# A graph network stack on one core: the ranking stage's lists carry two f32 values per node in place of five bf16 values

## The chip, the cores and the metric

The kernel runs on one core of a Trainium2 chip, as one launch. The metric is the device time of that core in microseconds (us), read as the median of several executions. The core has five engines with instruction streams of their own: TensorE (PE, matmuls; its weight loads are shown apart as PEld), VectorE (DVE), ScalarE (ACT), GpSimd (POOL) and SyncE (SP, which here issues transfers). Each works through its own stream in order and waits on semaphores of the others.

## The reference

Four graph layers with residuals over 2708 nodes with 128 features. Only the second layer matters here:

```python
h = jnp.maximum(_layernorm(x, axis=-1), 0.0)
x = x + _L1_gnn_ref(h, adj, L1_gnn_W, L1_gnn_a)

def _L1_gnn_ref(X, A, W, a):
    XW = jnp.matmul(X, W)
    f = W.shape[1]
    s_col = jnp.matmul(XW, a[0, :f])
    s_row = jnp.matmul(XW, a[0, f:])
    Z1 = jax.nn.leaky_relu(s_row[:, None] + s_col[None, :], negative_slope=0.01)
    den = jnp.exp(Z1)
    num = jnp.matmul(A, den)
    att = jnp.where(num != 0, den / jnp.where(num != 0, num, 1.0), 0.0)
    H = jnp.matmul(A, jnp.matmul(att, XW))
    return H
```

`num` is a product of two 2708 x 2708 matrices, but `den` depends on a pair of nodes only through the sum of two numbers, and the leaky ReLU has one kink. So for a column the rows fall into two groups, those whose `s_row` is above minus `s_col` and those below. If the rows are sorted by `s_row`, `num` follows from running sums over the sorted rows.

## The kernel before

The 2708 nodes are T = 22 tiles of P = 128 (the last has 20). The kernel runs layer 0, then the **ranking stage** of layer 1, then the **knots stage** (running sums over sorted rows of the adjacency, written to a table in DRAM), then a stage that gathers pairs of table rows and forms the attention, then layers 2 and 3. Almost every instruction around the change goes through `pe`, `dve` or `act` (line 86), wrappers that keep an engine's instructions in the order of the text; in the profile they all carry line L84, so groups are told apart by their tiles. The order of the ranking stage is thus written out by hand, in the loop at lines 1527 to 1572.

**The ranking stage.** `row_all` holds all nodes' row terms along the free axis, `r_nat` the same numbers by tile and partition. For tile `t`:

- `mask(t)` (DVE, line 1344) writes a bf16 mask of the nodes behind this one whose term is not larger. `masks` live in `flags`, a pool of three buffers, so `mask(t)` waits until `counts(t-3)` and `summed(t-3)` have read theirs.
- `counts(t)` (PE, line 1379) adds the mask's columns into the PSUM tiles `cnt`, 512 columns a bank, with bf16 matmuls of 32 columns of ones.
- `summed(t)` (ACT, line 1372) adds the mask along its row into `later`, writing a copy that nobody reads into `seen`; three tiles (2, 19, 20) do it on DVE inside `mask`.
- Every four tiles `count_row(b)` (ACT) copies a finished bank's row out of PSUM, `count_turn(b)` (PE) turns it into a column by four transposes, and `ranked(b)` (DVE) forms the rank of each node of the group, after the column is there.
- `listed(t0, t1)` (DVE, line 1454) turns ranks into a tile number and a place in that tile and writes, per node, a one-hot row over tiles (`in_tile`, 22 wide), a one-hot row over places (`in_place`, 131 wide) and the first multiplied by the node's values `vals` (`in_tile_v`). They are held in `in_spare` for tiles 0 to 15 (eight at a time) and in the buffer `lists` for tiles 16 to 21.
- `joined(t0, t1)` (PE, line 1482) multiplies, for each tile, the one-hot places (as weights) with `in_tile_v`, and adds into the PSUM tile `sp`: this scatters each node's values to its rank. It does so in two matmuls a tile: one whose weights are the last three columns of `in_place` (`DUP`; they carry knots to the next tile's start) and one whose weights are the first 128.
- `totals(n)` (PE, line 1251) takes the next `n` row tiles of the adjacency and adds their weighted rows, as f32 matmuls with 32 weight columns, eight a tile. This is a separate sum over all rows that needs no ranking; its tiles are spread over the loop by the table `TOTALS`, and the last one is done after `weights(0)` (line 1663).

A value is an f32 number, so before the change it is carried as bf16 pieces: the node number as partition and tile (`vals` 0 and 1), and the row term `r_n` as three bf16 terms whose sum is the number (`vals` 2 to 4, made on POOL by `split_terms`, line 1518). `sp` has `LIST = 5 * T = 110` columns and starts from `empty`, constants for the places that no node fills.

**Behind the loop** (lines 1564 to 1572): `listed(12, 16)`, `ranked(4)`, `listed(16, 20)`, `count_row(5)`, `count_turn(5)`, `ranked(5)`, `listed(20, T)`, `joined(12, T)`. Then DVE puts the pieces together into `src_u` (which row of the adjacency comes at which place) and `rs` (its row term), and POOL's queue gathers the adjacency's rows in sorted order: `fetch(t)` (line 1604), an indirect transfer of 1354 KB a tile into `mov`. POOL computes nothing of weight here; its queue holds these gathers in order. `rs` goes through three exponentials on ACT into the weights `wt` of the knots stage.

**The knots stage** (line 1755) multiplies each gathered tile with `wt`, copies the result to SBUF and writes it to `table`; SP issues those writes, and `fetch(t + 3)` the gather of a later tile.

Of the kernel before, what the change touches and what calls it, by code (L numbers as in the profile page):

```python
# [17 lines left out]
P = 128  # L18
# [6 lines left out]
def kernel(  # L25
# [18 lines left out]
    nc = tc.nc  # L44
    N, D = x.shape
    assert D == P
    T = -(-N // P)
# [25 lines left out]
    def pin(ins):  # L73

        return tc.keep_in_program_order(ins)
# [188 lines left out]
    nc.vector.memset(at_place[:, P + 2 :], float(PER))  # L264
    at_tile = consts.tile([P, T], F32, name="at_tile")
    nc.gpsimd.iota(at_tile, [[1, T]], base=0, channel_multiplier=0, allow_small_or_imprecise_dtypes=True)
    own_id = consts.tile([P, T], F32, name="own_id")
    nc.gpsimd.iota(own_id, [[0, T]], base=0, channel_multiplier=1, allow_small_or_imprecise_dtypes=True)
    vals = consts.tile([P, 5, T], BF16, name="vals")
    nc.vector.tensor_copy(vals[:, 0, :], own_id)  # L270
    nc.vector.tensor_copy(vals[:, 1, :], at_tile)
    empty = consts.tile([P, 5, T], BF16, name="empty")
    nc.vector.memset(empty, 0.0)
    for v, first, fill in ((1, 3, float(P // 2)), (2, 2, -1e5)):
        nc.gpsimd.affine_select(
            out=empty[:, v, :], in_=empty[:, v, :], pattern=[[0, T]],
            compare_op=ALU.is_ge, fill=fill, base=-first, channel_multiplier=1,
        )
        nc.gpsimd.affine_select(
            out=empty[:, v, :], in_=empty[:, v, :], pattern=[[-PER, T]],  # L280
            compare_op=ALU.is_ge, fill=fill, base=N + 2, channel_multiplier=-1,
        )
    nc.vector.scalar_tensor_tensor(
        empty[:, 2, 0:1], ident[:, 2:3], 88.0, empty[:, 2, 0:1], op0=ALU.mult, op1=ALU.add
    )
    source = consts.tile([P, 2], F32, name="source")
    nc.vector.tensor_scalar(
# [355 lines left out]
    for c in range(len(COLS) - 2):  # L643
        t0, t1 = COLS[c]
# [331 lines left out]
    def vec(name, n=T, dt=F32):  # L976
        return keep.tile([P, n], dt, name=name)
# [215 lines left out]
    nc.gpsimd.memset(later[:, T - 1 :], 0.0)  # L1193
    nc.gpsimd.memset(rank[:, T - 1 :], 0.0)
    hi, rmax, part = vec("hi", 1), vec("rmax", 1), vec("part", 1)
    r_n, w_n = vec("r_n"), vec("w_n")
    sp = acc(4)
    LIST = 5 * T
    q0, e4, e5 = KBS[E3][0], range(*GROUPS[E4]), range(*GROUPS[E5])
    copy_h(E3 - 1, last_turn[0])  # L1200
    roots(E3)
# [70 lines left out]
    def front_total():  # L1272
# [5 lines left out]
    totals(1)  # L1278
    terms_turned(E3 - 1)
    pe.matmul(  # L1280
        sp[:, :LIST], ident_b, empty.rearrange("p v t -> p (v t)"), start=True, stop=False
    )
    rows_p = ps_s.tile([P, 512], F32, name="ps")
    turn_h(E3, rows_p)
# [49 lines left out]
    cnt = [ps_s.tile([P, 512], F32, name="ps") for _ in range(2)]  # L1334


    lists = lay.tile([P, 2 * N], BF16, name="lists", tag="H")
    seen = lists[:, :N]

    SUMMED_HERE = (2, T - 3, T - 2)  # L1340
    own_later = {t: vec(f"own_later{t}", 1) for t in SUMMED_HERE}
# [30 lines left out]
    def summed(t):  # L1372
        w, a = width(t), t * P
        if t not in SUMMED_HERE:
            act.activation(
                seen[:w, a:], masks[t][:w, a:], AF.Copy, accum_out=later[:w, t : t + 1]
            )
# [55 lines left out]
    def in_spare(first):  # L1433
        box(
            first,
            8,
            (
                spare.tile([P, 8, T], BF16, name="in_tile"),
                spare.tile([P, 8, P + 3], BF16, name="in_place"),
                spare.tile([P, 5, 8, T], BF16, name="in_tile_v"),  # L1440
            ),
        )

    def in_lists(first, n):
        o = N
        made = []
        for shape, size in (("(i t) -> i t", n * T), ("(i t) -> i t", n * (P + 3)), ("(v i t) -> v i t", 5 * n * T)):
            kw = dict(i=n) if shape[1] == "i" else dict(v=5, i=n)
            made.append(lists[:, o : o + size].rearrange("p " + shape.replace("-> ", "-> p "), **kw))
            o += size  # L1450
        assert o <= 2 * N
        box(first, n, made)

    def listed(t0, t1):

        n = t1 - t0
        (ta, pl, tv), i = boxes[t0]
        r_, a_, m_ = rank[:, t0:t1], tile_of[:, t0:t1], at_of[:, t0:t1]
        dve.tensor_scalar(a_, r_, -(PER + 1) / 2.0, 1.0 / PER, op0=ALU.add, op1=ALU.mult)
        dve.tensor_scalar(a_, a_, 1.5 * BIG, None, op0=ALU.add)  # L1460
        dve.tensor_scalar(a_, a_, -1.5 * BIG, None, op0=ALU.add)
        dve.scalar_tensor_tensor(m_, a_, -float(PER), r_, op0=ALU.mult, op1=ALU.add)
        dve.tensor_tensor(
            ta[:, i : i + n, :],
            at_tile[:, None, :].to_broadcast([P, n, T]),
            a_[:, :, None].to_broadcast([P, n, T]),
            ALU.is_equal,
        )
        dve.tensor_tensor(
            pl[:, i : i + n, :],  # L1470
            at_place[:, None, :].to_broadcast([P, n, P + 3]),
            m_[:, :, None].to_broadcast([P, n, P + 3]),
            ALU.is_equal,
        )
        dve.tensor_tensor(
            tv[:, :, i : i + n, :],
            ta[:, None, i : i + n, :].to_broadcast([P, 5, n, T]),
            vals[:, :, t0:t1, None].to_broadcast([P, 5, n, T]),
            ALU.mult,
        )  # L1480

    def joined(t0, t1):
        for t in range(t0, t1):
            (_, pl, tv), i = boxes.pop(t)
            w = width(t)
            pe.matmul(
                sp[:3, :LIST].rearrange("p (v t) -> p v t", t=T)[:, 2:, 1:],
                pl[:w, i, DUP],
                tv[:w, 2:, i, : T - 1],
                start=False,  # L1490
                stop=False,
            )
            pe.matmul(
                sp[:, :LIST], pl[:w, i, :P], tv[:w, :, i, :], start=False, stop=(t == T - 1)
            )
# [19 lines left out]
        act.activation(s_n, c_n, AF.Exp, scale=0.99)  # L1515
        act.activation(sig, hb, AF.Exp)

    def split_terms():
        parts_of_r = keep.tile([P, 2, T], F32, name="parts_of_r")
        pin(nc.gpsimd.tensor_copy(vals[:, 2, :], r_n))  # L1520
        pin(nc.gpsimd.tensor_tensor(parts_of_r[:, 0, :], r_n, vals[:, 2, :], ALU.subtract))
        pin(nc.gpsimd.tensor_copy(vals[:, 3, :], parts_of_r[:, 0, :]))
        pin(nc.gpsimd.tensor_tensor(parts_of_r[:, 1, :], parts_of_r[:, 0, :], vals[:, 3, :], ALU.subtract))
        pin(nc.gpsimd.tensor_copy(vals[:, 4, :], parts_of_r[:, 1, :]))

    TOTALS = {6: 2, 7: 2, 10: 2, **{t: 1 for t in (0, 1, 2, 3, 8, 9, 12, 13, 14, 16, 18)}}
    for t in range(T):
        mask(t)
        if t == 1:
            split_terms()  # L1530
        if t == 7:
            ranked(0)
        if t == 8:
            column_max()
        if t == 10:
            ranked(1)
            in_spare(0)
            listed(0, 8)
        if t == 11:
            node_terms()  # L1540
        if t == 14:
            ranked(2)
            in_spare(8)
            listed(8, 12)
        if t == 18:
            ranked(3)
        counts(t)
        if t in (7, 11, 15):
            count_row(t // 4)
        summed(t)  # L1550
        if t == 4:
            front_total()
        if t in (3, 19):
            count_row(t // 4)
        if t % 4 == 0 and t:
            count_turn(t // 4 - 1)
        if t == 11:
            joined(0, 8)
        if t == 15:
            joined(8, 12)  # L1560
        if t in (2, 3, 4, 5):
            column_terms(t)
        totals(TOTALS.get(t, 0))
# [3 lines left out]
    listed(16, 20)  # L1567
    count_row(5)
    count_turn(5)
    ranked(5)  # L1570
    listed(20, T)
    joined(12, T)
# [6 lines left out]
    def signs_of(t):  # L1579
# [10 lines left out]


    src_u, rs = vec("src_u", dt=U32), vec("rs")
    ids = vec("ids")
    dve.tensor_copy(ids, sp[:, :T])
    dve.scalar_tensor_tensor(
        src_u, sp[:, T : 2 * T], float(P), ids, op0=ALU.mult, op1=ALU.add
    )
    dve.tensor_copy(rs, sp[:, 4 * T : 5 * T])
    dve.tensor_tensor(rs, sp[:, 3 * T : 4 * T], rs, ALU.add)
    dve.tensor_tensor(rs, sp[:, 2 * T : 3 * T], rs, ALU.add)  # L1600

    moving = {}

# [32 lines left out]
    nc.vector.tensor_copy(wt[:, :, 0], pw)  # L1636
    nc.vector.tensor_copy(wt[:, :, 1], nw)

    below = spare.tile([P, 4, P], F32, name="below", tag="below")
    for g in range(4):  # L1640
        dve.tensor_copy(below[:, g, :], ident[:, 32 * g : 32 * g + 1].to_broadcast([P, P]))
    dve.memset(below[:, :, 0:1], 0.0)
# [390 lines left out]
```

## Time and profile before

| what | value |
|---|---|
| median of 3 runs | 1090.12 us (1088.93 to 1092.9) |
| the profiled execution: its own time | 1095.87 us |
| the profiled execution: span of its instructions | 1094.2 us |
| mean granted TensorE clock in it | 0.968 of full speed |
| PE busy over the span | 994.4 us (91%), 3561 instructions |
| DVE, ACT, POOL busy | 586.0, 402.8, 214.1 us |
| moved by DMA | 282.72 MB, 258 GB/s over the span |
| ranking loop to the first gather of the knots stage | about 416 us to 463.8 us of the span |

The profiled execution is a single one and is 5.75 us longer than the median of the three that were timed; differences of a microsecond are read inside it, not between it and the others. In the profile an f32 matmul appears as two MATMUL records (and two weight loads), a bf16 matmul and a transpose as one. A timeline row merges neighbouring instructions of one kind: start, length, engine, line, operation, the tiles written and read, shapes (weights' rows and columns, then partitions by moving columns), how many records, and in brackets how long the engine was idle before it and what ended that.

### The profile page before, as it was taken

To read this page: it belongs to the slowest core of one execution; us is meant where nothing else is said; L and a number is where in the kernel's file an instruction comes from. 1 tells how busy PE (TensorE), PEld (TensorE's weight loads), DVE (VectorE), ACT (ScalarE), POOL (GpSimd) and SP (SyncE) were. 2 spreads that over 40 slices of the span, in tenths; PEclk is the share of its full clock that TensorE was granted. 3 is DMA by queue.
4 is the path that set the end of the run, shared out by engine and by line. 5 is a ranking of instruction groups with operands and counts; after the bars stand their busy time and mean duration, and the time that the engine had idled before them with its cause. 6 is when DMAs were issued, how large, how long until landed. Compare 5 with 4: busy or idle time off the path is not lost.

```text
span 1094.2 us, 10202 instructions
## 1 busy us (share of the span) xinstructions
PE 994.4 (91%) x3561; PEld 486.0 (44%) x3561; DVE 586.0 (54%) x1208; ACT 402.8 (37%) x637; POOL 214.1 (20%) x242
## 2 busy tenths in 40 slices
PE   6999999999899999899798288778999999999998
PEld 5445444444344445554343133333444545554444
DVE  4365368999863276856475499989300311031003
ACT  5100045544300058579675377878100310021000
POOL 2000000000188741023232155551000000000000
PEclk9999999999999998999999669999999999999999
DMA  9987220004399439399999899998999167716801
GB/s 272 347 318 234 89 68 16 0 1 153 123 363 405 159 128 413 143 382 425 419 421 388 308 431 431 432 431 350 425 352 410 75 229 279 255 51 224 301 36 51
DMA packets 48083, 282.72 MB, mean 258 GB/s; under 512 B 6238, under 2 KB 17594, under 8 KB 28420
## 3 DMA queue, kind: packets, MB, share of 16 engines
q1 hardware_dynamic: 38191, 189.13, 45.9%
q0 software_dynamic: 9840, 92.94, 20.9%
q8 instruction: 28, 0.46, 0.2%
q14 instruction: 24, 0.20, 0.0%
HBM read 250.06 MB, written 33.00 MB: 259 GB/s over the span
## 4 chain that ended last, share of the span: by engine, by line
PE 64%; DMA 22%; DVE 8%; ACT 2%; issue 2%; POOL 1%; SPq 0%; DVEq 0%; POOLq 0%; ACTq 0%
PE acc L404 31%; PE acc L84 16%; DMA pair<-table,pair_u 11%; PE acc L806 10%; DMA mov<-in_adj_dram,src_u 6%; DMA chunk<-in_adj_dram 3%; DVE att L84 3%; PE ps L84 3%; PE ps L384 1%; DVE top_i L843 1%; DMA held<-in_adj_dram 1%; PE acc L814 1%; ACT sg L1582 1%; DVE mov L84 1%; DMA w<-in_L_gnn_W_dram 1%
## 5 line engine op out<-in xcount | busy, mean ns | idle before, releaser
L84 PE MATMUL acc<-att,xw 128*128 128x512 f32 (+3 forms) x264 | 111.6, 577 | 51.4 <-DVE att L84 51.4
L404 PE MATMUL acc<-chunk,h 128*128 128x512 f32 (+1 forms) x384 | 148.0, 542 | 0.0
L84 PE MATMUL acc<-mov,wt 128*128 128x512 f32 (+1 forms) x264 | 111.0, 568 | 18.1 <-DVE mov L84 16.1
L806 PE MATMUL acc<-zT 128*128 128x512 f32 (+2 forms) x264 | 112.3, 559 | 0.0
L404 PEld LDWEIGHTS acc<-chunk,h 128*128 128x128 f32 x384 | 68.8, 190 | 74.1 <-issue 74.1
L84 PEld LDWEIGHTS acc<-att,xw 128*128 128x128 f32 (+1 forms) x264 | 50.6, 199 | 112.4 <-issue 81.8
L947 POOL DMA_INDIRECT gath<-ydr,near_u x63 | 60.3, 957 | 154.4 <-DMA ydr<-y 140.6
L84 PEld LDWEIGHTS acc<-mov,wt 128*128 128x128 f32 x264 | 48.0, 194 | 80.5 <-DVE mov L84 39.8
L404 PE MATMUL acc<-chunk,y 128*128 128x512 f32 x204 | 80.0, 553 | 3.8 <-DMA chunk<-in_adj_dram 3.0
L821 ACT COPY strip<-acc 128x512 f32<-128x512 f32 (+1 forms) x132 | 60.4, 560 | 59.2 <-issue 35.8
L1805 POOL DMA_INDIRECT pair<-table,pair_u x22 | 66.6, 3026 | 75.7 <-DVE att L84 63.8
L84 DVE SCALAR_TENSOR_TENSOR att<-pair,kap 128x2708 f32<-128x2708 f32 (+3 forms) x28 | 67.7, 2433 | 23.1 <-DMA pair<-table,pair_u 23.1
L84 DVE COPY mov<-knots 2x512 f32<-2x512 f32 x126 | 47.6, 402 | 51.1 <-DMA mov<-in_adj_dram,src_u 25.8
L404 PE MATMUL acc<-chunk,attended 128*128 128x512 f32 x192 | 73.6, 543 | 0.4 <-DMA chunk<-in_adj_dram 0.4
L84 ACT ACTIVATE att<-att,sca 128x2708 f32<-128x2708 f32 (+3 forms) x28 | 57.8, 2065 | 37.6 <-DVE att L84 37.6
L823 DVE MAX8 top_v<-strip 128x8 f32<-128x2708 f32 (+1 forms) x22 | 64.7, 2966 | 7.3 <-ACT strip L821 7.3
L806 PEld LDWEIGHTS acc<-zT 128*128 128x128 f32 (+1 forms) x264 | 45.1, 185 | 51.3 <-issue 43.8
L84 DVE SCALAR_TENSOR_TENSOR att<-row_all,inv_s,att 128x2708 f32<-128x2708 f32 (+3 forms) x28 | 67.6, 2428 | 0.4 <-ACT att L84 0.4
L84 ACT ACTIVATE att<-att,hb 128x2708 f32<-128x2708 f32 (+3 forms) x28 | 57.9, 2068 | 0.9
L404 PEld LDWEIGHTS acc<-chunk,y 128*128 128x128 f32 x204 | 37.2, 193 | 45.8 <-issue 41.3
L1582 ACT ACTIVATE sg<-row_all,c_nat 128x2708 bf16<-128x2708 f32 (+1 forms) x22 | 56.4, 2564 | 0.1
L84 ACT COPY knots<-acc 128x512 f32<-128x512 f32 x66 | 37.3, 594 | 42.0 <-PE acc L84 40.8
(381 smaller groups left out, 1267.2 us busy)
## 6 DMA issues: line engine op xcount, KB each, us to landing
chunk<-in_adj_dram SPq DMA_DIRECT2D x75, 1354.0 KB
table<-knots SPq DMA_DIRECT2D x19, 1354.0 KB
res<-in_adj_dram SPq DMA_DIRECT2D x9, 1354.0 KB
held<-in_adj_dram SPq DMA_DIRECT2D x11, 512.0 KB
held<-in_adj_dram SPq DMA_DIRECT2D x16, 256.0 KB
upper<-in_adj_dram SPq DMA_DIRECT2D x4, 842.0 KB
held<-in_adj_dram SPq DMA_DIRECT2D x3, 1024.0 KB
chunkY<-in_adj_dram SPq DMA_DIRECT2D x2, 1354.0 KB
```

The source lines that it names most:

```text
L84: return lambda *a, **k: pin(getattr(self.engine, name)(*a, **k))
L384: mm = nc.tensor.matmul(p[: width(t), t - t0, :], srcT[:, cols(t)], w, start=True, stop=True)
L404: nc.tensor.matmul(out[b][:, :n], y[r, tile_at(i), :], chunk(i)[r, k0 : k0 + n], start=(i == 0), stop=(i == T - 2),)
L806: mm = nc.tensor.matmul(zz[b][:w, :n], zT[:, cols(t)], zT[:, k0 : k0 + n], start=True, stop=False)
L814: nc.tensor.matmul(zz[b][:w, :n], ones_b[g : g + 3, :w], sq_rows[g : g + 3, k0 : k0 + n], start=False, stop=True,)
L821: copied = nc.scalar.copy(s[:w, k0 : k0 + n], zz[b][:w, :n])
L823: nc.vector.max(top_v[:w, t, :], s[:w, :])
L843: pin(nc.vector.max_index(top_i[:w, t, :], top_v[:w, t, :], strips[t][:w, :]))
L947: nc.gpsimd.indirect_dma_start(out=g[: idx.shape[0], :], out_offset=None, in_=ydr[:, :], in_offset=bass.IndirectOffsetOnAxis(ap=idx, axis=0),)
L1582: nc.scalar.activation(sg[:w, :], row_all[:w, :], AF.Sign, bias=c_nat[:w, t : t + 1], accum_out=signs[:w, t : t + 1],)
L1805: nc.gpsimd.indirect_dma_start(out=r[:w].rearrange("p a n -> p (a n)"), out_offset=None, in_=table[:, :], in_offset=bass.IndirectOffsetOnA ...
```

## The change

- **Values.** `vals` becomes two f32 numbers per node: the node number `128 t + p`, made by one iota, and `r_n`, which is now written in place (`r_n = vals[:, 1, :]`). `split_terms` and the two copies and the iota that made the bf16 pieces are gone. `empty` and `LIST` shrink with it (2 x 22 = 44 columns of f32 in place of 110 of bf16).
- **Lists.** `in_tile`, `in_place` and `in_tile_v` are f32; `lists` keeps its bytes, its lower half now holds the f32 lists and its upper half `seen`. `in_place` and the later `below` share a buffer.
- **Matmuls.** `joined` and the matmul that starts `sp` are f32 matmuls: 44 and 21 moving columns in place of 110 and 63.
- **Behind it.** `src_u` is one DVE instruction on PSUM (it adds 0.25 before the conversion) in place of two, `rs` one copy in place of a copy and two additions.
- **Order.** `count_row(2)` and `count_row(3)` stand behind `summed(11)` and `summed(15)` in ACT's order, where they stood ahead; `count_row(1)` stays ahead. The totals tile that was taken at t = 18 is taken behind `count_turn(5)`, ahead of `ranked(5)`, `listed(20, T)` and `joined(12, T)` in the text. SP's order of transfers is the same.

```diff
-    vals = consts.tile([P, 5, T], BF16, name="vals")
-    nc.vector.tensor_copy(vals[:, 0, :], own_id)
-    nc.vector.tensor_copy(vals[:, 1, :], at_tile)
-    empty = consts.tile([P, 5, T], BF16, name="empty")
+    vals = consts.tile([P, 2, T], F32, name="vals")
+    nc.gpsimd.iota(vals[:, 0, :], [[P, T]], base=0, channel_multiplier=1, allow_small_or_imprecise_dtypes=True)
+    empty = consts.tile([P, 2, T], F32, name="empty")
...
-    r_n, w_n = vec("r_n"), vec("w_n")
+    r_n, w_n = vals[:, 1, :], vec("w_n")
     sp = acc(4)
-    LIST = 5 * T
+    LIST = 2 * T
...
-        sp[:, :LIST], ident_b, empty.rearrange("p v t -> p (v t)"), start=True, stop=False
+        sp[:, :LIST], ident, empty.rearrange("p v t -> p (v t)"), start=True, stop=False
...
-    lists = lay.tile([P, 2 * N], BF16, name="lists", tag="H")
-    seen = lists[:, :N]
+    lists = lay.tile([P, N], F32, name="lists", tag="H")
+    seen = lists[:, N // 2 :].bitcast(BF16)
+    wide = lists[:, : N // 2]
...
-                spare.tile([P, 8, T], BF16, name="in_tile"),
-                spare.tile([P, 8, P + 3], BF16, name="in_place"),
-                spare.tile([P, 5, 8, T], BF16, name="in_tile_v"),
+                spare.tile([P, 8, T], F32, name="in_tile"),
+                spare.tile([P, 8, P + 3], F32, name="in_place", tag="in_place"),
+                spare.tile([P, 2, 8, T], F32, name="in_tile_v"),
...
-            ta[:, None, i : i + n, :].to_broadcast([P, 5, n, T]),
-            vals[:, :, t0:t1, None].to_broadcast([P, 5, n, T]),
+            ta[:, None, i : i + n, :].to_broadcast([P, 2, n, T]),
+            vals[:, :, t0:t1, None].to_broadcast([P, 2, n, T]),
...
-                sp[:3, :LIST].rearrange("p (v t) -> p v t", t=T)[:, 2:, 1:],
+                sp[:3, T + 1 : LIST],
                 pl[:w, i, DUP],
-                tv[:w, 2:, i, : T - 1],
+                tv[:w, 1, i, : T - 1],
...
-    TOTALS = {6: 2, 7: 2, 10: 2, **{t: 1 for t in (0, 1, 2, 3, 8, 9, 12, 13, 14, 16, 18)}}
+    TOTALS = {6: 2, 7: 2, 10: 2, **{t: 1 for t in (0, 1, 2, 3, 8, 9, 12, 13, 14, 16)}}
     for t in range(T):
         mask(t)
-        if t == 1:
-            split_terms()
...
         counts(t)
-        if t in (7, 11, 15):
+        if t == 7:
+            count_row(1)
+        summed(t)
+        if t in (11, 15):
             count_row(t // 4)
-        summed(t)
...
     count_row(5)
     count_turn(5)
+    totals(1)
     ranked(5)
     listed(20, T)
     joined(12, T)
...
-    ids = vec("ids")
-    dve.tensor_copy(ids, sp[:, :T])
-    dve.scalar_tensor_tensor(
-        src_u, sp[:, T : 2 * T], float(P), ids, op0=ALU.mult, op1=ALU.add
-    )
-    dve.tensor_copy(rs, sp[:, 4 * T : 5 * T])
-    dve.tensor_tensor(rs, sp[:, 3 * T : 4 * T], rs, ALU.add)
-    dve.tensor_tensor(rs, sp[:, 2 * T : 3 * T], rs, ALU.add)
+    dve.tensor_scalar(src_u, sp[:, :T], 0.25, None, op0=ALU.add)
+    dve.tensor_copy(rs, sp[:, T:LIST])
...
-    below = spare.tile([P, 4, P], F32, name="below", tag="below")
+    below = spare.tile([P, 4, P], F32, name="below", tag="in_place")
```

More of the change, by code (lines that the diff above doesn't have):

```diff
@@ L266 @@
     nc.gpsimd.iota(at_tile, [[1, T]], base=0, channel_multiplier=0, allow_small_or_imprecise_dtypes=True)
-    own_id = consts.tile([P, T], F32, name="own_id")
-    nc.gpsimd.iota(own_id, [[0, T]], base=0, channel_multiplier=1, allow_small_or_imprecise_dtypes=True)
-    vals = consts.tile([P, 5, T], BF16, name="vals")
-    nc.vector.tensor_copy(vals[:, 0, :], own_id)
-    nc.vector.tensor_copy(vals[:, 1, :], at_tile)
-    empty = consts.tile([P, 5, T], BF16, name="empty")
+    vals = consts.tile([P, 2, T], F32, name="vals")
+    nc.gpsimd.iota(vals[:, 0, :], [[P, T]], base=0, channel_multiplier=1, allow_small_or_imprecise_dtypes=True)
+    empty = consts.tile([P, 2, T], F32, name="empty")
     nc.vector.memset(empty, 0.0)
-    for v, first, fill in ((1, 3, float(P // 2)), (2, 2, -1e5)):
+    for v, first, fill in ((0, 3, float(P * P // 2)), (1, 2, -1e5)):
         nc.gpsimd.affine_select(
@@ L283 @@
     nc.vector.scalar_tensor_tensor(
-        empty[:, 2, 0:1], ident[:, 2:3], 88.0, empty[:, 2, 0:1], op0=ALU.mult, op1=ALU.add
+        empty[:, 1, 0:1], ident[:, 2:3], 88.0, empty[:, 1, 0:1], op0=ALU.mult, op1=ALU.add
     )
@@ L1444, in in_lists @@
     def in_lists(first, n):
-        o = N
+        o = 0
         made = []
-        for shape, size in (("(i t) -> i t", n * T), ("(i t) -> i t", n * (P + 3)), ("(v i t) -> v i t", 5 * n * T)):
-            kw = dict(i=n) if shape[1] == "i" else dict(v=5, i=n)
-            made.append(lists[:, o : o + size].rearrange("p " + shape.replace("-> ", "-> p "), **kw))
+        for shape, size in (("(i t) -> i t", n * T), ("(i t) -> i t", n * (P + 3)), ("(v i t) -> v i t", 2 * n * T)):
+            kw = dict(i=n) if shape[1] == "i" else dict(v=2, i=n)
+            made.append(wide[:, o : o + size].rearrange("p " + shape.replace("-> ", "-> p "), **kw))
             o += size
-        assert o <= 2 * N
+        assert o <= N // 2
         box(first, n, made)
@@ L1516, in node_terms @@
         act.activation(sig, hb, AF.Exp)
[L1518 to L1524, printed above, removed]
-    TOTALS = {6: 2, 7: 2, 10: 2, **{t: 1 for t in (0, 1, 2, 3, 8, 9, 12, 13, 14, 16, 18)}}
+    TOTALS = {6: 2, 7: 2, 10: 2, **{t: 1 for t in (0, 1, 2, 3, 8, 9, 12, 13, 14, 16)}}
     for t in range(T):
         mask(t)
-        if t == 1:
-            split_terms()
         if t == 7:
```

## The prediction

> **What bounds the kernel now.** I read the page first (PE is busy 91% of the span, so anything that PE gets to do is suspect), then the windows around the change, then the chain that ended last, then the timelines of PE and DVE between 416 and 468 us. Each windows row has the stretch, its length, the busy time and instructions of PE, PEld, DVE, ACT and POOL, the granted TensorE clock, the DMA share and GB/s.
>
> ```profile
> 443.00:454.00 11.00, 11.00 (x134) 6.93 (x130) 8.72 (x31) 8.50 (x17) 0.00 (x0) 1.00 0.40 150
> 454.00:464.00 10.00, 5.31 (x48) 3.19 (x40) 8.19 (x41) 2.07 (x9) 0.23 (x1) 0.81 0.00 0
> 464.00:492.00 28.00, 26.87 (x106) 14.52 (x107) 16.67 (x47) 19.02 (x28) 8.00 (x8) 0.94 0.94 369
> 492.00:520.00 28.00, 26.13 (x84) 13.05 (x83) 18.44 (x52) 25.35 (x30) 10.41 (x10) 1.00 1.01 425
> ```
>
> From 443 to 454 us PE is never idle (nor in the timeline from 417 on); from 454 to 464 it is idle half the time and DVE is busy; DMA is idle there and then full from 464 on. The chain (start, length, what) says the same:
>
> ```profile
> 452.13 1.68 PE acc L84 x20
> ...
> 454.09 0.17 DVE mask L84
> ...
> 461.68 0.78 PE acc L84 x4
> ...
> 462.69 0.18 DVE src_u L84
> ...
> 463.77 4.50 DMA mov<-in_adj_dram,src_u
> ```
>
> So the stage has two parts: a PE part, released to DVE at 454.1 when `counts(17)` frees a mask buffer, and a DVE part from `mask(20)` to `src_u`, in which PE only fills in. Then the first gather opens a stage that DMA fills: a later `src_u` makes everything behind it later by as much, an earlier one earlier.
>
> **The dear term: a tile of `joined` on PE.** The rows that price it:
>
> ```profile
> 443.72 2.30 PE L84 MATMUL acc<-in_tile_v,in_place 128*3 128x63 bf16 x16
> 445.94 0.39 PE L84 MATMUL ps<-mask,ones_b 128*32 128x512 bf16 x3
> 421.64 1.05 PE L1078 MATMUL acc<-wga,h1T 128*128 128x1 f32 x8
> 422.62 1.35 PE L84 MATMUL acc<-res,w_a 128*32 128x338 f32 x16
> 29.38 0.61 PE L84 MATMUL ps<-quarters,totals 128*128 128x1 f32 x4 [0.46 <-ACT totals L84]
> 29.85 1.43 PE L84 MATMUL acc<-w,h0T 128*128 128x128 f32 x7
> 309.59 0.19 PE L928 MATMUL ps<-ones,owns 128*1 128x1 f32 x2
> 309.70 0.24 PE L930 MATMUL ps<-of_four,ident 20*32 20x2 f32 x8
> ```
>
> Now: eight tiles from 443.72 to 445.94, 2.22 / 8 = 0.278 us a tile. After: no row has this pair in f32, so it is put together. The f32 matmuls with 128 weight columns and one moving column take 0.47 for 4 records when the next group also has 128 columns (29.38 to 29.85) and 0.98 for 8 when the next has 32 (421.64 to 422.62): so 0.112 to 0.118 a record, set by the weight load, and 0.98 - 8 x 0.112 = 0.085 for changing the width. A totals tile (eight matmuls, 16 records, four at a time) takes 452.47 to 453.65 = 1.18, so a round of four 338-column records about 0.29, or 0.87 ns a moving column; 44 columns add 0.037 to the last record. The 128-column matmul of a tile: 2 x 0.112 + 0.037 + 0.085 = 0.35. The 3-column one: one-column weights took 309.59 to 309.70 = 0.11 for both records, change of width included; 2 x 21 columns add 0.03: 0.14. Together x = **0.49 us** a tile against 0.278. Bounds: 0.28 if nothing is paid for the changes of width and the narrow records take 0.03 each (2 x 0.112 + 0.06); 0.65 if the narrow ones cost like wide ones (2 x 0.112 + 0.085 + 0.35). I take 0.49, since its parts come from rows of the same weight widths.
>
> [...]
>
> **The change, part by part.**
>
> 1. Twelve tiles are joined before 454 us, where PE has no gap: 12 x (0.49 - 0.278) = **+2.55**. `mask(20)` waits there for PE:
>
> ```profile
> 454.08 0.35 DVE L84 SCALAR_TENSOR_TENSOR mask<-row_all,r_nat,above 128x128 bf16<-128x128 f32 x1 [0.32 <-PE ps L84]
> 456.15 0.61 DVE L84 TENSOR_TENSOR in_tile_v<-in_tile,vals 128x440 bf16<-128x440 bf16 x1
> 457.44 0.21 PE L84 MATMUL acc<-ident,row 1*128 1x1 f32 x2 [0.78 <-DVE rank L84]
> ```
>
> 2. `in_tile_v` for four tiles shrinks from 440 to 176 elements: the next instruction follows 0.53 after it (456.15 to 456.68); 176 elements (`in_tile` of eight tiles, 439.49 to 439.74) take 0.25: **-0.28** ahead of `ranked(4)`, and so of `count_turn(5)`, which waits for its read. The other two lists gain 0.28 and 0.15 more. [...]
>
> 3. From `count_turn(5)` (457.44) to `src_u` (462.69) it takes 5.25 now. After, PE has 0.15 of transposes, the moved totals tile 1.18, ten tiles 10 x 0.49 = 4.90, and 0.10 of drain and issue (four tiles last 1.18 now, where 4 x 0.278 is 1.11, and the chain has 0.02 behind them): 6.33, **+1.08**. The copy `ids` (0.21) is gone in this. DVE's lists for tiles 20 and 21 would be ready at 461.68 - 0.71 + 2.55 = 463.5, PE comes to them at 465.0: PE, which waited 0.78, 0.69 and 0.97 us here, becomes the bound, and the savings of step 2 beyond 0.28 go into DVE's waiting.
>
> 4. Where the totals tile stood, between `counts(18)` and `counts(19)`, PE was ahead of `ranked(4)` by a DVE list; taking it away there gives 0, and without it the 1.18 would stand in the PE part's tail and still not delay `mask(20)`. Its load was issued at 433.5 on SP, whose order does not change; no other queue is passed.
>
> 5. The count rows behind the sums: ACT stops waiting for PE (2.64 us before row 2, 1.37 before row 3) and frees masks earlier; DVE waited 0.61 and 1.06 for that. It then waits for PE at `mask(20)` instead: 0. Row 3 is copied when PE has it (450.77) or `summed(15)` is done, about 450.9, and its transposes come at 452.1 or later; if that cover of 0.7 were gone, its lateness would add one to one.
>
> 6. At zero: the setup (two small DVE copies and an iota less, while the chain lies in PE and the first loads), `split_terms` (POOL, 416.4 to 419.0; POOL's next work is at 431.6), the f32 start of `sp` (PE then waits for ACT until 408.0), `rs` ready 0.4 earlier (its weights are needed only when the gather has landed at 468.3), `below` in `in_place`'s buffer (written at 464.5, after the last read that `src_u` itself waits for; uncovered it would cost its 0.8).
>
> **Sum.** 2.55 - 0.28 + 1.08 = **+3.35 us**, or for any tile cost x: 12(x - 0.278) - 0.28 + (1.43 + 10x - 5.25) = 22x - 7.43. That is 1095.87 + 3.35 = 1099.2 for the profiled execution; this lies 5.75 above the median, 1090.12, and the same addition puts the median at **1093.5**.
>
> **Rivals.**
>
> *A. PE keeps its pace, and DVE's end comes first: faster.* If the f32 pair costs no more than 0.28 (decided below x = 0.29), the PE part is unchanged, PE meets the last lists, and DVE's savings count: 0.71 of lists, 0.21 of `ids`, 0.1 since two tiles run at full clock: -1.0, **1089.1**. For: consecutive bf16 matmuls with 128 columns follow each other at 0.056 us (four `parts` records, 152.51 to 152.73), so 0.278 for a pair shows exposed loads, which f32 might hide. Against: the pair changes width as before.
>
> *B. The clock halves in the new tail: slower, at its far end past the bound.* The granted clock was 0.5 from 429.5 to 436.4 and from 460.3 to 467.1, each time after a stretch of few or short matmuls. With the totals tile gone from 454 to 455, PE is sparse for longer before `count_turn(5)` at 459.7, and the work put behind it is longer. At half clock I double both: a tile 0.98, the totals tile 2.36. If the clock halves at 460.3 for 3.4 us: the totals tile ends at 461.8, two tiles by 463.7, eight more by 467.6: +5.0, **1095.1**; for 6.8 us: +6.7, **1096.8**. It decides once the half clock falls into that PE-bound tail. Against: the place of these stretches need not repeat in another execution.
>
> [...]
>
> *C. The delay is absorbed behind the gather.* Then **1090.1**. For: at 464 to 492 DMA is at 0.94, not full. Against: PE waits 0.72 us for that gather at 468.8, and DMA is at 1.01 in the next stretch.
>
> **Chances.** Forecast (x from 0.4 to 0.56, full clock or nearly, +1.4 to +4.9): 0.46. B: 0.27. A: 0.12. C: 0.12. Something else: 0.03. Half a per cent, 5.45 us, is about what a measurement of this kernel can tell from no change. It is passed by the upper part of B and by the dear end of x (22 x 0.65 - 7.43 = +6.9): 0.22. Faster by as much would need what no case gives: 0.03. The rest, 0.75, lies within. The range reaches from A (1089.1) to B's far end with a little for the spread of the runs (3.97 us in three): 1089.2 to 1097.2.
>
> **What would show it.** After: `joined`'s eight tiles last about 3.9 us instead of 2.2; `mask(20)` starts some 2.5 us later relative to the loop's start; between `count_turn(5)` and `src_u` PE has no gap; no DVE wait on ACT before `mask(18)`; the first gather is later by the sum and the gather stage as long as before. I am wrong if a tile takes below 0.35, if PE idles before the last lists, or if `mask(20)` is released by something else.

## The result, and the profile after

| | median | runs |
|---|---|---|
| before | 1090.12 us | five, 1087.82 to 1092.9 |
| after | 1101.95 us | five, 1099.43 to 1103.57 |
| after / before | 1.0081 | 95% interval 1.0055 to 1.0108 |

The change makes the kernel slower by some 8.8 us (0.0081 x 1090.12; 6.0 to 11.8 by the interval). The ratio on record is not the quotient of the two five-run medians, which would be 1.0109, or 11.8 us; the twelve runs of the changed kernel in e1 below give 1.0078, so the text goes by the ratio. The forecast, +3.35 us, is below the interval, and the predicted range ended at 1097.2 us.

I read the trace of after at the places that the prediction named, by landmarks. From the first `joined` record to `mask(20)` (the PE part) before took 454.08 - 443.72 = 10.36 us and after 14.54; from `mask(20)` to the first gather's issue (the tail) 463.77 - 454.08 = 9.69 and 13.21. So 20.05 us became 27.75, **+7.70**. From that issue to the end of the span it is 630.4 us before and 630.3 after. In these two traces the loss thus lies in these 28 us; how far that holds for other executions is said with what stays open. The two spans differ by 3.5 us only, 1097.7 and 1094.2, mostly because the mask loop ahead (from the first mask to the first joined record) took 34.84 us in before's profiled execution and 31.58 in after's; why is told in the last section. In the same windows as before (the clock is the third number from the end):

```profile
443.00:454.00 11.00, 11.00 (x113) 7.34 (x113) 5.38 (x22) 4.81 (x13) 0.00 (x0) 0.84 0.27 109
454.00:464.00 10.00, 7.68 (x57) 5.37 (x53) 6.09 (x33) 1.15 (x4) 0.00 (x0) 0.71 0.00 0
464.00:492.00 28.00, 25.45 (x108) 14.27 (x109) 13.69 (x42) 16.16 (x28) 7.59 (x8) 0.86 0.81 315
```

The granted clock was 1.00, 0.81 and 0.94 in these windows before; now it is 0.84, 0.71 and 0.86. The timeline of PE in after:

```profile
439.66 3.96 PE L84 MATMUL acc<-in_tile_v,in_place 128*3 128x21 f32 x32
...
444.21 2.13 PE L84 MATMUL acc<-chunk,w_n 128*32 128x338 f32 x16
...
449.99 2.01 PE L84 MATMUL acc<-in_tile_v,in_place 128*3 128x21 f32 x16
...
452.59 1.35 PE L84 MATMUL acc<-chunk,w_n 128*32 128x338 f32 x16
...
457.24 0.21 PE L84 MATMUL acc<-ident,row 1*128 1x1 f32 x2 [1.63 <-DVE rank L84]
457.39 1.67 PE L84 MATMUL acc<-chunkY,w_n 128*32 128x338 f32 x16
458.81 3.10 PE L84 MATMUL acc<-in_tile_v,in_place 128*3 128x21 f32 x16
461.84 4.54 PE L84 MATMUL acc<-lists 128*3 128x21 f32 x24
```

Eight tiles take 3.9 us, four 1.95: 0.49 us a tile, as forecast. But a totals tile that takes 1.35 us at 452.59 takes 2.13 at 444.21, and four tiles that take 1.95 at 449.99 take 3.03 (458.81 to 461.84) in the tail: those pieces ran at half clock. In windows of 1 us the half clock lies at 444 (444.6) for 3.4 us, just behind the eight tiles, and from 458 (458.3) for 13.7 us, of which 8.1 us come before `src_u`. The chain of waits and DVE's timeline of after show who sets the end of the tail:

```profile
456.94 0.17 DVE rank L84
457.11 0.14 issue
457.24 9.16 PE acc L84 x57
466.42 0.18 DVE src_u L84
```

```profile
450.27 0.35 DVE L84 SCALAR_TENSOR_TENSOR mask<-row_all,r_nat,above 128x128 bf16<-128x128 f32 x1 [0.66 <-PE ps L84]
...
460.77 0.24 DVE L84 TENSOR_TENSOR lists<-lists,vals 128x88 f32<-128x88 f32 x1
466.42 0.18 DVE L84 TENSOR_SCALAR src_u<-acc 128x22 uint32<-128x22 f32 x1 [5.41 <-PE acc L84]
```

Before, the chain's step ahead of `src_u` was 0.78 us of PE behind DVE's list; now it is 9.16 us of PE without a gap, and DVE, done with its lists at 461.0, waits 5.41 us. At 450.27 DVE waits for PE, no longer for ACT.

### The profile page after: what moved, and what is told of

The parts are those of the page before. It is cut to its first block, busy times and chain, and to the rows that moved or that the text cites. A ratio compares the mean times of both kernels' runs of the same rounds, so it can differ in the third digit from the quotient of the medians.

```text
span 1097.7 us, 10281 instructions
## 1 busy us (share of the span) xinstructions
PE 1000.2 (91%) x3606; PEld 492.8 (45%) x3606; DVE 583.5 (53%) x1203; ACT 402.9 (37%) x637; POOL 212.4 (19%) x237
## 4 chain that ended last, share of the span: by engine, by line
PE 66%; DMA 22%; DVE 6%; issue 3%; ACT 2%; POOL 0%; SPq 0%; POOLq 0%; DVEq 0%; ACTq 0%
PE acc L401 31%; PE acc L84 18%; DMA pair<-table,pair_u 10%; PE acc L803 10%; DMA mov<-in_adj_dram,src_u 7%; DMA chunk<-in_adj_dram 3%; PE ps L84 3%; DVE att L84 2%; PE ps L381 1%; DVE top_i L840 1%; DMA held<-in_adj_dram 1%; PE acc L811 1%; DMA w<-in_L_gnn_W_dram 1%; ACT sg L1573 1%; PE acc L1075 0%
```

## The experiments

Every ratio is against the kernel before on the same chip; each kernel ran twelve times unless said otherwise, the kernel before 27 to 35 times. "PE part" and "tail" are the two stretches above, from each kernel's one trace, with their sum against before's 20.05 us.

| kernel | PE part | tail | sum, less 20.05 | ratio, 95% interval |
|---|---|---|---|---|
| changed, again (e1) | 14.54 | 13.26 | +7.75 | 1.0078 [1.0051, 1.0106] |
| lists only (e2) | 12.86 | 10.18 | +2.99 | 1.0048 [1.0017, 1.0078] |
| order only (e3) | 10.36 | 10.74 | +1.05 | 1.0001 [0.9981, 1.0021] |
| changed, grouped by width (e4) | 10.73 | 10.30 | +0.98 | 1.0027 [1.0004, 1.0050] |
| before, again (e5) | 10.36 | 9.70 | +0.01 | 1.0003 [0.9974, 1.0033] |
| before, grouped (e6) | 9.24 | 9.79 | -1.02 | 0.9996 [0.9972, 1.0019] |
| changed, dense fill in the tail (e7) | 14.54 | 11.32 | +5.81 | 1.0042 [1.0016, 1.0067] |
| lists only, grouped (e8) | 10.72 | 9.53 | +0.20 | 1.0017 [0.9993, 1.0041] |
| order, dense pad a tile (e9) | 12.94 | 13.26 | +6.15 | 1.0040 [1.0014, 1.0066] |
| order, thin pad a tile (e10, six runs) | 12.49 | 11.94 | +4.38 | 1.0081 [1.0051, 1.0111] |
| dense pad, again (e13, eleven runs) | 12.95 | 14.44 | +7.34 | 1.0072 [1.0042, 1.0102] |
| thin pad, again (e14) | 12.48 | 13.80 | +6.23 | 1.0066 [1.0038, 1.0094] |
| changed, dense behind eight tiles (e15) | 14.59 | 12.94 | +7.48 | 1.0064 [1.0035, 1.0093] |
| changed, grouped and fill (e11) | 10.73 | 9.05 | -0.27 | 1.0010 [0.9985, 1.0034] |
| before, grouped and fill (e12) | 9.25 | 9.78 | -1.02 | 0.9975 [0.9949, 1.0001] |
| the same, again (e16) | 9.24 | 9.63 | -1.18 | 0.9982 [0.9956, 1.0009] |

### The parts of the change (e1 to e4)

My theory after the result, H: the f32 tiles cost what the sum says at full clock, and the rest is half clock that they bring. Rivals: L, the half clock was luck of one execution; O, the order of the totals tile and the count rows costs the time.

The changed kernel unedited:

> The changed kernel once more, for a second trace and a second comparison. Theory H (half clock): the profiled execution of the changed kernel lost 7.7 us between its first list matmul (439.7) and the first gather (467.4) against the one of before (443.7 to 463.8), of which 3.3 us are the f32 tiles at full clock and the rest half-clock stretches in and behind the list matmuls; so this trace again shows half clock right behind the eight joined tiles and in the tail, and the ratio is 1.007 to 1.011. Theory L (luck): the 1.1% is the spread of two sessions; the ratio comes nearer to 1.003 (+3.4 us).

Measured 1.0078, and a trace with the half clock at the same two places (444 for 3.4 us, 457 for 13.7 us). L falls.

The f32 lists, with the order of before:

```diff
-    TOTALS = {6: 2, 7: 2, 10: 2, **{t: 1 for t in (0, 1, 2, 3, 8, 9, 12, 13, 14, 16)}}
+    TOTALS = {6: 2, 7: 2, 10: 2, **{t: 1 for t in (0, 1, 2, 3, 8, 9, 12, 13, 14, 16, 18)}}
...
     count_turn(5)
-    totals(1)
```

> Only the f32 lists and values; the totals tile stays at t = 18 and the count rows stay ahead of the sums. Theory H: most of the loss is here: +5 to +9 us (tiles 12 x 0.21 on PE's path = 2.5, the rest half clock behind the longer list matmuls). Rival O (order): the loss comes from the order; then this is +2 us or less.

Measured 1.0048: 5.2 us (1.9 to 8.5 by the interval), the larger part by the middle values. Here no half clock fell into the PE part, and that grew by 12.86 - 10.36 = 2.50 us: the forecast's +2.55 for twelve tiles.

The order alone, with the bf16 lists (the converse edit):

> Only the order: the totals tile behind count_turn(5) and count rows 2 and 3 behind the sums, with the bf16 lists of before. Theory H: -0.5 to +2.5 us (PE has room in the tail for the 1.18 us; a half-clock stretch there can cost up to 2). Rival O: +5 us or more.

Measured 1.0001: O falls as a cause by itself. But e2 and e3 lengthen the tail by 0.49 and 1.05 us, the whole change by 3.5, more than the two together. PE's timelines show why, e2's first and then e3's:

```profile
451.88 2.02 PE L84 MATMUL acc<-in_tile_v,in_place 128*3 128x21 f32 x16
453.82 4.02 PE L84 MATMUL acc<-lists 128*3 128x21 f32 x24
...
454.65 1.53 PE L84 MATMUL acc<-in_tile_v,in_place 128*3 128x63 bf16 x8
456.11 2.18 PE L84 MATMUL acc<-lists 128*3 128x63 bf16 x12
```

No row has idle time ahead of it: with either part alone PE already goes without a gap from `count_turn(5)` to `src_u`, 6.1 us in each, and DVE waits for it at the end (2.38 and 1.93 us). Before, PE waited 0.69 and 0.96 us there for DVE's lists. Either part alone is paid largely out of these waits; with both there is no more to pay from, and PE needs 9.2 us. The two halves of the order were not tried apart.

Last, the changed kernel with each group's 3-column matmuls first and its 128-column ones behind, so that the weights change width twice a group and not twice a tile:

```diff
-            (_, pl, tv), i = boxes.pop(t)
+            (_, pl, tv), i = boxes[t]
             w = width(t)
             pe.matmul(
                 sp[:3, T + 1 : LIST],
...
             )
+        for t in range(t0, t1):
+            (_, pl, tv), i = boxes.pop(t)
+            w = width(t)
             pe.matmul(
...
-    joined(12, T)
+    joined(12, 16)
+    joined(16, 20)
+    joined(20, T)
```

> The changed kernel with the same list matmuls in another order: for each group of tiles first all narrow (3-column) ones, then all wide ones; so the weight width changes twice a group in place of twice a tile. If the cost of a tile (0.49 us) is the change of width and the load exposed by it, eight tiles take about 2.4 us in place of 3.9 and the kernel gains 12 x 0.19 = 2.3 us on PE's path and up to 1.9 us in the tail: -3 to -5 us against the changed kernel, more if half-clock stretches go with it. If the width has no part in it, nothing changes.

Its timeline of PE:

```profile
440.14 2.47 PE L84 MATMUL acc<-in_tile_v,in_place 128*3 128x21 f32 x32
...
447.31 1.38 PE L84 MATMUL acc<-in_tile_v,in_place 128*3 128x21 f32 x16
```

The same 32 records take 2.4 us in place of 3.9, 0.30 us a tile, and the ratio falls to 1.0027. So 0.19 us of the f32 tile goes with its two changes of weight width.

### Control, fill and grouping elsewhere (e5 to e8)

The kernel before, again:

> The kernel before, run once more as its own control and for a second trace of it. All theories: ratio 1.000 within 0.3%. The question is what its tail looks like in another execution. Theory H (sparse or slow PE work sets off the half clock, and f32 tiles make the stretch longer) expects at most 6.8 us of half clock between the first joined tile and the gather, and joined-to-gather near 20 us as in the first trace (18 to 22). Theory L (the place of the stretches is luck, whatever the kernel) would allow 13.7 us here too, and then 23 us or more.

Ratio 1.0003 and 20.06 us from first tile to gather, as expected. The half clock lay from 456 (456.3) for 10.2 us, longer than in the first trace; 3.7 us of it lie ahead of the gather, within the 6.8 allowed there. Its windows and its PE timeline:

```profile
455.00:458.00 3.00, 1.41 (x10) 0.81 (x9) 2.55 (x13) 0.00 (x0) 0.00 (x0) 0.72 0.00 0
458.00:461.00 3.00, 1.46 (x7) 1.03 (x7) 2.09 (x13) 0.49 (x3) 0.95 (x1) 0.50 0.00 0
```

```profile
455.73 1.32 PE L84 MATMUL acc<-lists 128*3 128x63 bf16 x8 [0.69 <-DVE lists L84]
457.95 0.77 PE L84 MATMUL acc<-lists 128*3 128x63 bf16 x4 [0.90 <-DVE lists L84]
```

PE is idle half the time there and waits for DVE's lists. Of what the half clock lengthens there, DVE waits for the last two tiles alone: 0.77 us, where at full clock half of the four tiles' 1.18 (at 453.86) is 0.59. This changed the theory: **the half clock in the tail is not new. The kernel before has it too; there DVE's pace hides nearly all of it, and the change lets PE set the pace in it.** The amount is not the same: from `mask(20)` to `src_u` it is 2.4 and 2.6 us in the two traces of before, 8.1 and 8.3 in those of the changed kernel. All eighteen traces (both kernels as first run, and these sixteen) have 3.4 to 17.1 us of half clock between 450 and 475 us.

The kernel before, grouped by the same edit:

> The kernel before (bf16 lists, old order) with the joined matmuls of a group reordered: all 3-column ones, then all 128-column ones. Theory W (a tile's cost is half the change of weight width, 0.085 to 0.1 us twice a tile) expects eight tiles in about 1.2 to 1.5 us instead of 2.2, twelve tiles 1.2 us less ahead of mask(20); behind it DVE sets the pace, so 1 to 1.5 us in all, ratio 0.9985 to 0.999. If the shorter PE part leaves PE sparser and the clock halves once more (H), nothing or a small loss: 1.000 to 1.002. If f32 alone pays for the change of width and bf16 does not: tile still 0.278, 1.000.

```profile
443.33 0.92 PE L84 MATMUL acc<-in_tile_v,in_place 128*3 128x63 bf16 x16
...
449.79 0.59 PE L84 MATMUL acc<-in_tile_v,in_place 128*3 128x63 bf16 x8
```

Eight tiles take 0.9 us in place of 2.2, less than the 1.2 to 1.5 expected; the stretch is 1.02 us shorter, and the ratio, 0.9996, can't tell that from nothing.

The changed kernel with eight dense dead matmuls (512 moving columns, bf16) where PE idles ahead of its new tail:

```diff
+        if t == 20:
+            filler = acc(5)
+            warm(filler, 2)
         counts(t)
...
     count_row(5)
+    warm(filler, 6)
     count_turn(5)
```

> The changed kernel with eight extra 512-column bf16 matmuls on PE, into an accumulator nobody reads: two before counts(20), six between the count row of group 5 and its transposes, where PE is thin. It only adds PE work. Theory H (the half clock in the tail follows thin PE work) expects the 13.7 us of half clock between 457 and 472 to shrink to 0 to 6.8, and src_u to come 1.5 to 3 us earlier after the first joined tile than in the changed kernel: 1.005 to 1.007 against the kernel before. The theory that only the f32 records' length counts expects the added work to cost 0 to 2 us: 1.008 to 1.010.

Its timeline of PE:

```profile
456.22 1.47 PE L312 MATMUL acc<-ident_b 128*128 128x512 bf16 x6
457.92 0.21 PE L84 MATMUL acc<-ident,row 1*128 1x1 f32 x2 [0.23 <-DVE rank L84]
458.07 1.35 PE L84 MATMUL acc<-chunkY,w_n 128*32 128x338 f32 x16
459.24 2.02 PE L84 MATMUL acc<-in_tile_v,in_place 128*3 128x21 f32 x16
461.18 3.99 PE L84 MATMUL acc<-lists 128*3 128x21 f32 x24
```

PE does 1.7 us more work and the kernel is faster than the changed one, 1.0042. The totals tile and four tiles are back at 1.35 and 2.02 us, the half clock begins at 462 and lasts 6.8 us, and the tail is 1.9 us shorter. Work that only kept PE occupied gave time back here, somewhat more than expected; the ratios' intervals still overlap a little. The trace shows what it took away: of half clock between `mask(20)` and `src_u` 3.0 us are left where the changed kernel had 8.1.

The f32 lists in the old order, grouped, which makes the cheap f32 tile of the prediction's rival A:

> f32 lists, totals at t = 18 and count rows ahead of the sums as before, joined matmuls grouped by width. This makes the cheap f32 tile (0.30 us) of rival A. If A's condition decides, DVE's end comes first and the time is that of the kernel before or 1 us under it: 0.999 to 1.000. Theory H with half clock behind any f32 tile expects 2 to 4 us more: 1.002 to 1.004. The summed order (totals moved) was worth nothing with bf16 lists, so this should not differ by more than 1 us from the grouped changed kernel if order is worth nothing with f32 lists too.

The stretch, 20.25 us, is that of before within 0.2. DVE sets the pace again up to its lists of tiles 16 to 19, for which PE waits 0.22 us at 454.4; from there PE needs 3.7 us, almost all at half clock (454.7 for 10.2 us), and DVE waits 1.72 us for it. So DVE's end does not come first here, and a tile of 0.30 us is just above A's 0.29. The ratio, 1.0017 [0.9993, 1.0041], doesn't separate the two expectations, but A's gain of 1.0 us (0.9991) lies just outside.

### Dense against thin (e9, e10, e13, e14)

Is it the tile's length or its kind? With bf16 lists and the order of the change, a dead matmul was put behind every joined tile: dense (one bf16 matmul, 512 columns) or thin (one f32 matmul, one column). N below is the theory that only length counts.

```diff
     def joined(t0, t1):
+        pad = acc(5)
...
+            warm(pad, 1)
```

The thin one has this in place of the last line:

```diff
+            pe.matmul(pad[:, :1], ident, ident[:, :1], start=True, stop=True)
```

> bf16 lists as before, totals and count rows in the order of the change, and behind every joined tile one dead bf16 matmul with 512 moving columns into an accumulator nobody reads: 0.21 us more a tile, so PE's time for a tile is that of the f32 one (about 0.49 us), but dense work. Theory H (length by itself costs the forecast's +3.4 us; the rest of the +8.8 is half clock, set off by thin PE work) expects 1.002 to 1.004 and a mean granted clock not below the kernel before (0.969). Theory N (only the length of the tiles counts, and it is worth the whole 8.8 us through what is queued behind) expects 1.007 to 1.009.

> As the dense one, but the dead work behind every joined tile is one f32 matmul with 128 weight columns and a single moving column: two records of 0.11 us, so again 0.22 us a tile, of thin work. Theory H expects 1.006 to 1.009, a mean granted clock below the kernel before (0.967 or less), and more half clock between the first joined tile and the gather than in the dense one. Theory N expects the same as the dense one, within 0.002.

> The dense dead work once more. Theory H (half clock set off by thin PE work): 1.002 to 1.005, mean granted clock at or above the kernel before. Theory N (only length counts): the same as the thin one beside it.

> The thin dead work once more, its tile a little shorter than the dense one (0.456 us against 0.494). Theory H: 1.006 to 1.009, at least 0.002 above the dense one, mean granted clock below the kernel before. Theory N: equal to or below the dense one.

The first pair, 1.0040 and 1.0081, looked like H; the second, 1.0072 and 1.0066, doesn't. In time the two kinds are **not told apart**. The mean granted clock over the runs differs, 0.9694 and 0.9684 with dense pads against 0.9668 and 0.9655 with thin ones (0.001 is 2 x 0.001 x 1094 = 2.2 us of half clock), but the thin tile is shorter (0.456 us, eight from 434.88 to 438.53, against 0.494). Nor do the traces tell them apart: from the first joined record to the gather they have 6.8 and 10.2 us of half clock with dense pads, 5.2 and 10.8 with thin ones. What both pairs show fits the theory after e5: PE is the bound of the tail in all four, and the tail has half clock whatever the tile is made of. A dense pad adds 0.494 - 0.278 = 0.22 us a tile, 22 x 0.22 = 4.8 us of PE at most, and the four traces have a tail 2.3 to 4.8 us longer than before's.

### The half clock at 444 us (e15)

In the three traces of kernels with the ungrouped f32 tiles and the moved totals (after, e1, e7) a half clock of 3.4 us began 4 to 5 us after the first joined record. Dense work behind those eight tiles alone:

```diff
-    def joined(t0, t1):
+    def joined(t0, t1, pad=None):
...
+            if pad is not None:
+                warm(pad, 1)
...
-            joined(0, 8)
+            joined(0, 8, acc(5))
```

> The changed kernel with one dense dead matmul (512 columns, bf16, 0.21 us) behind each of the first eight tiles only, 1.7 us more work where PE has no gap. Theory H: the half clock that follows these eight tiles (at 444 to 448 us in three traces, 1.7 us lost) is gone from the trace, the eight tiles take 5.6 us, and the time is that of the changed kernel: 1.007 to 1.009. Theory N: half clock stays where chance puts it, and the time grows by the 1.7 us: 1.009 to 1.011.

Windows of after, then of this kernel:

```profile
440.00:444.00 4.00, 4.00 (x35) 3.02 (x35) 1.78 (x6) 3.91 (x8) 0.00 (x0) 1.00 1.00 371
444.00:448.00 4.00, 4.00 (x37) 2.56 (x40) 3.27 (x12) 1.05 (x4) 0.00 (x0) 0.58 0.49 200
```

```profile
444.00:448.00 4.00, 4.00 (x31) 2.43 (x30) 0.43 (x2) 2.80 (x6) 0.00 (x0) 1.00 0.85 341
448.00:452.00 4.00, 4.00 (x57) 2.77 (x59) 2.88 (x12) 0.18 (x1) 0.00 (x0) 1.00 0.07 26
452.00:456.00 4.00, 4.00 (x45) 2.74 (x41) 2.00 (x8) 3.47 (x9) 0.00 (x0) 1.00 0.00 0
```

The half clock is not there, the PE part is as long as after's (14.59 against 14.54) although it holds 1.7 us more work, and the ratio, 1.0064, is at or below the changed kernel's; that it would be 1.009 or more, as N has it, is at the edge of its interval. That the dense work removed it is not shown. Within a trace the half-clock stretches begin whole steps of 3.413 us apart (last section). Counted on from the others, a step begins 4.8 to 5.0 us behind the first joined record in the three traces that have the stretch, and 5.3 us behind it in e15. It is 5.3 in e2 too, which has the same tiles and no dense work, and no such stretch either. So the place of the tiles in the clock's rhythm explains e15 as well as the dense work does.

### Versions (e11, e12, e16)

Grouping and fill together, in the changed kernel and in the one before:

> The changed kernel with the joined matmuls grouped by width (tile 0.30 us) and the dense dead work in the tail (two matmuls before counts(20), six ahead of the last transposes). Each alone gave 5 us and 4 us back of 8.8. Theory H: both together 1.000 to 1.002, mean granted clock at or above 0.969. If both remove the same stretches of half clock: 1.002 to 1.004.

> The kernel before with grouped joined matmuls and the same dense dead work in the tail. DVE sets the pace in its tail, so H expects little from the clock there: 0.997 to 1.000, the mean granted clock above 0.969; the gain, if any, lies in the PE part (1.2 us) and in the first part of the gather stage. The theory that dead work costs its own time expects 1.001 to 1.002.

> The kernel before, grouped by width and with dense dead work in the tail, once more, to settle its sign. Theory H: 0.996 to 0.999, mean granted clock above 0.970. If the first reading was chance: 0.999 to 1.001.

The changed kernel so mended is at 1.0010 [0.9985, 1.0034]: the lower of the two expectations. Of 0.0078 it gives 0.0068 back, where e4's 0.0051 and e7's 0.0036 make 0.0087; the intervals don't tell these apart. In its trace 0.2 us of half clock are left between `mask(20)` and `src_u`. The kernel before so mended is the fastest of all, 0.9975 and 0.9982 on two chips. Each interval reaches 1; taken as independent their mean is 0.998, give or take 0.002. The traces show 1.0 to 1.2 us of it, in the PE part; where the rest lies, if it is there, they don't show.

## Why the prediction was wrong

1. **Tile price and PE part.** x = 0.49 was right. Two changes of width are 0.19 (e4); the sum had 0.085 for one and the other inside the narrow pair's 0.14. At full clock the twelve tiles cost 2.50 (e2) for 2.55. In after 1.68 came on top, the half clock at 444, which neither the sum nor a rival had (B has half clock in the tail alone).
2. **`in_tile_v`, -0.28.** Right: from `mask(20)` to `count_turn(5)` 3.36 us became 3.04.
3. **`count_turn(5)` to `src_u`, +1.08.** PE became the bound without a gap, as said, but it took 9.18 us and not 6.33: totals 1.42 for 1.18, four tiles 3.03 and six 4.54 for 4.90 together. The work was right, its clock was not: +2.85. **This is the step that failed**, with the forecast's condition, "full clock or nearly". The prediction had the half clock of 460.3 to 467.1 in its own trace, inside the tail that it handed to PE, and held against rival B that "the place of these stretches need not repeat". Half clock between 450 and 475 us repeated in every trace. A stretch that had cost next to nothing, because DVE was the bound in it, was read as luck rather than as cover.
4. **Totals away from t = 18, and the count rows.** Nothing in the PE part: e3 has 10.36 us there, to the hundredth that of before. DVE's waits for ACT went, as said; ACT's own did not all go, it still waits 1.96 us for PE ahead of row 3 (450.06). In the tail the move was not worth 0. Between `mask(20)` and `count_turn(5)` PE now waits 0.70 and 1.63 us (0.72 and 0.78 before), and the half clock begins earlier; this is rival B's condition. The windows in which it begins, in before, in e3 (the order alone) and in after:

```profile
460.00:461.00 1.00, 0.71 (x5) 0.36 (x4) 0.86 (x8) 0.00 (x0) 0.00 (x0) 0.65 0.00 0
...
451.00:452.00 1.00, 0.00 (x0) 0.00 (x0) 0.86 (x4) 0.00 (x0) 0.00 (x0) 0.90 0.00 0
...
458.00:459.00 1.00, 1.00 (x14) 0.35 (x6) 1.00 (x4) 0.00 (x0) 0.00 (x0) 0.64 0.00 0
```

   Behind `mask(20)` that is 6.2, 2.9 and 4.1 us. In the eighteen traces it begins 5.1 to 6.3 us behind `mask(20)` where the totals tile stands at t = 18 (five traces), 2.4 to 4.4 us where it was moved (nine), and 7.1 us or later where dense fill stands in the gap (four).
5. **Step 6 and rival C.** Nothing showed outside the stretch in after's trace (630.3 us behind it, 630.4 before), and nothing was absorbed there.
6. **Rival A** was refused by x = 0.49; with the tile of 0.30 us in e8 there was no gain to be seen, with half clock in the tail there too.
7. **Rival B** was the mechanism, at 0.27. Its far end, +6.7, was short of the 7.70 seen: it let the half clock begin at 460.3, where it began at 458.3 and covered the tail to its end, priced a slow tile at 0.98 where it is 0.757 (4.54 / 6), and left out the stretch at 444. By trace, +7.70 = 2.50 (tiles) + 1.68 (half clock at 444) + 3.52 (tail: the forecast's 0.8 and 2.7 of half clock). The interval of the ratio, 6.0 to 11.8 us, holds that.

What stays open: whether thin and dense tiles of one length differ in time; what exactly starts the half clock of the tail, which moved with PE's idle time and which no edit took wholly out of 450 to 475 us; whether the stretch at 444 comes from the f32 tiles or from their place in the clock's rhythm; and whether the change also costs something behind the gather. From the first gather's issue to the end, the two traces of before take 630.4 and 629.5 us, the two of the changed kernel 630.3 and 631.5, but e2 635.3 and e4 636.7. All eighteen lie between 629.4 and 638.5, the eight with f32 lists at 634.8 on average, the ten with bf16 lists at 631.1. The ratios of e2 and e4 stand for 5.2 and 3.0 us (1.9 to 8.5 and 0.4 to 5.5), 2 us more than their 28 us show; with intervals that wide this can't be settled.

## What to carry to other kernels

Before work is handed to an engine that so far only filled in, price it at the clock which the profile shows in that stretch, even if that clock cost little there until now. The matmuls here that alternate between narrow and wide weights paid 0.17 to 0.19 us a tile for their two changes (e4, e12), so order such matmuls by width first and only then ask what the type costs. Where PE idles just ahead of work that it bounds, a few dense dead matmuls can gain more than they cost (in e7 1.7 us of them made the tail 1.9 us shorter), and a trial of that kind helps to show whether the clock is the cause; one trace of it is not enough, since where the clock's steps fall differs between traces (4.8 to 5.0 us behind the first joined record in after, e1 and e7, 5.3 in e2 and e15).

## What the runs showed of the hardware

**In these traces the clock moves in steps of one length.** From the first mask to the first joined record the eighteen traces take 29.95, 31.6, 33.2 or 34.84 us, by 0, 1, 2 or 3 stretches of 3.4 us at half clock in it: 1.6 us each. In every trace the half-clock stretches begin whole multiples of 3.413 us apart (in before at 409.10, 429.58 and 460.30: 6 and 9 of them). Both traces of the kernel before had three, those of the changed one had one and two, which hid 1.7 to 3.3 us of the change's loss in its profiled runs. In after, PE is busy for 4.00 of 4.00 us from 440 to 444 at clock 1.00 and for 4.00 of 4.00 from 444 to 448 at 0.58, half clock from 444.6 on. So here PE lost its clock although the profile shows it busy.

**The change of width is a large part of a joined tile's price.** A bf16 tile falls from 0.278 to about 0.11 us when grouped (eight tiles, 441.57 to 442.42 in e12), an f32 one from 0.49 to 0.30: 0.17 to 0.19 us for two changes with either type, about as much as the f32 type itself costs (0.30 - 0.11 = 0.19 grouped, 0.49 - 0.278 = 0.21 not).
